# Two graph layers, a mixture of experts and a grouped attention: the weights and masks of the heads built inside the second graph, four open tails, and another last tile

## The chip, the cores and the metric

The kernel runs on one core of a Trainium2 chip. The metric is the device time of one execution in microseconds (us), the median of several runs. The engines have short names in the profile: PE is TensorE (matrix products; PEld is its weight load), DVE is VectorE, ACT is ScalarE, POOL is GpSimd, SP is SyncE, which here only issues transfers. [...]

## The reference, cut to what matters

Input x has 3327 rows of 256 numbers; adj is a 3327 x 3327 matrix of zeros and ones. Everything is float32.

```python
# layer 0
x = x + _L0_gnn_ref(_layernorm(x), adj, W, b)              # graph: normalised adjacency times features
x = x + _L0_ffn_ref(_layernorm(x)[None], ...)[0]           # 8 experts, the best 2 of each row
# layer 1
x = x + _L1_gnn_ref(_layernorm(x), adj, W, a)              # graph with attention weights
x = x + _L1_ffn_ref(_layernorm(x)[None], ...)[0]           # the heads
```

The second graph computes `softmax(where(adj > 0, leaky_relu(e_src + e_dst), -9e15)) @ (x @ W)`. The heads (`_L1_ffn_ref`, 4 heads, 4 queries each, called "experts" e in the kernel, 64 wide):

```python
sx = einsum('bsh,ndh->bnsd', x, hl_w) + hl_b
pad = sx == 0
q = einsum('bnsd,neod->bneso', sx, wq);  k = ... wk;  v = ... wv
att = softmax(einsum('bnesd,bntd->bnest', q, k) * d ** 0.5 + causal)
qkv = where(pad, 0, einsum('bnest,bntd->bnesd', att, v))
gs = softmax(einsum('bnsf,nef->bnse', out, gate_w) + gate_b)      # out is qkv, laid side by side
mixed = einsum('bnsed,bnse->bnsd', out, gs)
hn = layernorm(mixed + resid, ln_g, ln_b)                          # resid is sx
hx = where(pm, 0, relu(where(pm, 0, fx @ fc1.T + fc1_b)))          # fx is hn, pm is fx == 0
hx = layernorm(where(pm, 0, hx @ fc2.T + fc2_b) + fx, fnorm_g, fnorm_b)
fg = softmax(fout @ fgate_w.T)                                     # fout is hx of the four heads
return fout * fg
```

## The kernel before, in words

Rows are cut into 26 tiles of 128. The kernel runs four stages one after the other: the first graph with the experts beside it, the second graph (`graph1`, line 482, until about 974 us of the span), and the heads (`heads`, line 773, from there to the end, 3070.9 us).

**Order.** In the second graph and the heads, instructions are issued through `InOrder` (lines 45 to 100): it adds to each instruction a dependency on the one before it on the same engine. So each engine runs them in the order in which the program writes them, and no scheduler changes that. Since every such instruction is recorded at line 61, the profile's groups are told apart by tile names and shapes.

**The second graph.** Seven blocks of up to four output tiles; a block goes through 26 steps j, one for each source tile. In a step DVE makes u (the larger of two shifted score rows) and p (u masked by the adjacency panel pan), ACT the exponential between them, and PE multiplies p with wh into the accumulators acc. Panels (`panel`, line 668) are fetched by SP, four source tiles at a time; on the diagonal POOL adds the identity (pan<-pan rows). The panel that a step needs is asked for eight steps earlier. POOL also makes the small matrices dg for the next block. Block 3 is the one from about 790.4 to 846.4 us of the span. `finish` (line 712) divides, adds the residual and writes a tile of x to DRAM (xs) through POOL's queue.

**The heads, setup.** At lines 787 to 799 thirteen small weights are loaded with `Net.load` (line 118), which issues on ACT's queue. At lines 810 and 814 twelve parts of wk and wq are loaded on SP's queue. igw, the matrix that turns a head's output back and makes its gate logits, is built by POOL: 32 copies of a 64x64 identity (line 822), and eight transfers of the gate weights on ACT's queue (line 823). own and after, which put the causal mask on the diagonal through a product, are made by POOL's memsets and affine selects (`where`, line 833).

**The heads, loop.** `prepare` (line 880), a generator, makes what a tile t needs: its row norm (xres, prs, xn), the transpose xt, the product sx (psxt in PSUM), then sxd, v, kt, the queries qt and sx. A unit is a tile t and a head h; a unit's keys come in t // 4 + 1 groups g of up to four tiles, and a unit with a group is a chunk. For each chunk: `fill` (PE: scores pqk), `drain` (DVE: from PSUM into sc, with the maximum), `weigh` (ACT: exponential with sum), `values` (SP: loads vr), `turn` (DVE: transposes sc), `attend` (PE: sc times vr into po). After a unit's last group, `over` (line 1074) copies po (ACT) and multiplies by sxd (POOL); in the next chunk `back` (line 1084) makes ptO and fills the head's part of qkv and glp. A running sum of the costs of ACT and DVE (`load`) decides in `empty` (line 856) which of these two makes certain copies out of PSUM.

After head 3, `back` opens the tile's tail (`tail`, line 1146), another generator, which runs in 17 steps between the chunks of later tiles: gate softmax and reciprocals (DVE, ACT), mix of the four experts and residual into fx (POOL), `norm4` (statistics on DVE, power and the rest on POOL), transpose, the two small products ph (PE), mask and sum fo (DVE, POOL), second `norm4`, transpose, pfg and the last softmax, product and sum with x (POOL), output. The main loop (lines 1271 to 1288) advances each open tail and each open `prepare` by one step per chunk, through `run` (line 964); from tile 8 on it leaves out the chunk after a unit's end. Before a tail is opened, open ones are advanced until at most two are left:

```python
                if h == 3:
                    while len(tails) > 2:
                        run(tails)
                    tails.append(tail(u["t"], u["sx"], r["qkv"], r["glp"], r["den"]))
```

At the end, `back(ended)` and `while tails: run(tails)` (lines 1294 and 1295) finish the last tile.

Of the kernel before, what the change touches and what calls it, by code (L numbers as in the profile page):

```python
# [12 lines left out]
F32 = mybir.dt.float32  # L13
BF16 = mybir.dt.bfloat16
# [3 lines left out]
AF = mybir.ActivationFunctionType  # L18
ALU = mybir.AluOpType
AX = mybir.AxisListType  # L20
PSUM = bass.MemoryType.PSUM

P = 128
N = 3327
NT = 26
NP = NT * P
D = 256
# [3 lines left out]
NEG = -1e30  # L31
# [70 lines left out]
class Net:  # L102
# [15 lines left out]
    def load(self, pool, src, shape, name, eng=None, bufs=None):  # L118
        t = pool.tile(shape, F32, name=name, tag=name, bufs=bufs)
        (eng or self.nc.scalar).dma_start(out=t, in_=src)  # L120
        return t

    def load_rows(self, pool, vec, n, name, bufs=None):

        return self.load(pool, vec.partition_broadcast(P), [P, n], name, bufs=bufs)
# [353 lines left out]

        return beside  # L480

    def graph1(self, xs, made):
        tc, a, x = self.tc, self.a, self.x
        nc = InOrder(tc)
        HP = NP // 2

        PARTS = ((0, HP, HP + 9 * P, NP), (0, HP, NP))
        with ExitStack() as ctx:
            one = ctx.enter_context(tc.tile_pool(name="g1", bufs=1))
            panp = ctx.enter_context(tc.tile_pool(name="g1pan", bufs=3))  # L490
            first = ctx.enter_context(ExitStack())
            ps = first.enter_context(tc.tile_pool(name="g1ps", bufs=2, space=PSUM))
# [251 lines left out]
            weights(1)  # L744
            masked(0)
            for k, (b, j) in enumerate(steps):
                if k + 8 in when:
                    load(*when[k + 8])
                if k + 2 < len(steps):
                    if steps[k + 2][1] % 4 == 0 and groups:  # L750
                        panel(*groups.pop(0))
                    weights(k + 2)
                if k + 3 in when:
                    sign(*when[k + 3])
                if k + 1 < len(steps):
                    masked(k + 1)
                gather(k)
                if b and 1 <= j <= len(blocks[b - 1]):
                    finish(blocks[b - 1][j - 1])
                if k in when:  # L760
                    top(*when[k], PARTS[1])
                if b + 1 < len(blocks):
                    if j == 16:
                        dg = shifts(b + 1)
                    if j == 18:
                        pb = rows(b + 1, dg)
                    if j == 21:
                        spread_rows(b + 1, pb)
            for t in blocks[-1]:
                finish(t)  # L770


    def heads(self, xs, vs, out):
        tc, a = self.tc, self.a
        nc = InOrder(tc)
        Q = 32
        with ExitStack() as ctx:
# [6 lines left out]
            ps_o = ctx.enter_context(tc.tile_pool(name="pso", bufs=1, space=PSUM))  # L784
            ps = ctx.enter_context(tc.tile_pool(name="psm", bufs=4, space=PSUM))

            hlt = self.load(one, a["hlt"].rearrange("(k p) o -> p k o", p=P), [P, 2, D], "hlt")
            hlb = self.load(one, a["hlb"], [P, 2], "hlb")
            wv = self.load(one, a["wv"].rearrange("c p o -> p c o"), [P, 2, P], "wv")
            gb = self.load_rows(one, a["gateb"], 16, "gateb")  # L790
            lng = self.load_rows(one, a["lng"][:64], 64, "lng")
            lnb = self.load_rows(one, a["lnb"][:64], 64, "lnb")
            fc1 = self.load(one, a["fc1"], [P, P], "fc1")
            fb1 = self.load(one, a["fb1"], [P, 1], "fb1")
            fc2 = self.load(one, a["fc2"], [P, P], "fc2")
            fb2 = self.load_rows(one, a["fb2"][:64], 64, "fb2")
            fng = self.load_rows(one, a["fng"][:64], 64, "fng")
            fnb = self.load_rows(one, a["fnb"][:64], 64, "fnb")
            fgw = self.load(one, a["fgw"], [P, 2, 4], "fgw")

            wk = one.tile([P, 2, P], F32, name="wk")
            wq = one.tile([P, 2, 2, P], F32, name="wq")
            igw = one.tile([P, 4, 4, 68], F32, name="igw")
            for s in range(2):
                r = ds(64 * s, 64)
                for k in range(2):
                    self.nc.sync.dma_start(  # L810
                        out=wk[r, :, ts(k, 64)], in_=a["wk"][:, r, r].rearrange("c p o -> p c o")
                    )
                    for c in range(2):
                        self.nc.sync.dma_start(
                            out=wq[r, c, :, ts(k, 64)],
                            in_=a["wq"][c, k::2, r, r].rearrange("e p o -> p e o"),
                        )
            for k in range(2):
                r = ds(64 * k, 64)
                for e in range(4):  # L820
                    for h in range(4):
                        nc.gpsimd.tensor_copy(igw[r, h, e, :64], self.ident[r, r])
                    self.nc.scalar.dma_start(
                        out=igw[r, :, e, 64:], in_=a["gatew"][ds(64 * (e % 2), 64), :, e // 2, :]
                    )

            own = [one.tile([P, P], BF16, name=f"own{k}") for k in range(2)]  # L830
            after = [one.tile([P, P], BF16, name=f"after{k}") for k in range(2)]

            def where(t, op, base, sign=1):

                for k in range(2):
                    r = t[ds(64 * k, 64), :]
                    nc.gpsimd.affine_select(
                        out=r, in_=r, compare_op=op, fill=0.0, base=base,
                        pattern=[[sign, P]], channel_multiplier=-2 * sign,
                    )  # L840

            for k in range(2):
                nc.gpsimd.memset(own[k], 1.0)
                nc.gpsimd.memset(after[k], NEG)
            where(own[0], ALU.is_ge, 0)
            where(own[0], ALU.is_ge, 1, -1)
            where(after[0], ALU.is_ge, -2)
            where(own[1], ALU.is_equal, 0)
            where(after[1], ALU.is_equal, -1)

            kt = one.tile([P, 4, NP], F32, name="kt")

# [27 lines left out]
            def prepare(t, res):  # L880
# [14 lines left out]
                nc.vector.tensor_scalar(xn, x, mv[:, 0:1], rs, ALU.subtract, ALU.mult)  # L895
                load["dve"] += 0.35
                yield
                xt = self.work.tile([P, 2, P], F32, tag="xt", name="xt2")
                turned(xn, xt)
                yield  # L900
                pp = ps.tile([P, 2, P], F32, tag="b", name="psxt")
# [172 lines left out]
            def over(u):  # L1074

                u["ot"] = tl.tile([P, 4, P], F32, tag="ot", name="ot", bufs=1)
                nc.scalar.copy(u["ot"].rearrange("p e (q i) -> p q e i", q=4), po)
                nc.gpsimd.tensor_tensor(
                    u["ot"], u["ot"],
                    u["sxd"][:, u["h"] : u["h"] + 1, :].to_broadcast([P, 4, P]), ALU.mult,  # L1080
                )
                load["act"] += 0.6

            def back(u):


                h = u["h"]
                r = ready[u["t"]]
                if h == 0:
                    r["qkv"] = tl.tile([P, 4, 4, 64], F32, tag="qkv", name="qkv", bufs=2)  # L1090
                    r["glp"] = sm.tile([P, 4, 4, 4], F32, tag="glp", name="glp")
                pt = ps.tile([P, 4, 68], F32, tag="b", name="ptO")
                for e in range(4):
                    nc.tensor.matmul(
                        pt[:, e, :], u["ot"][:, e, :], igw[:, h, e, :], start=True, stop=True
                    )
                nc.scalar.copy(r["qkv"][:, h, :, :], pt[:, :, :64])
                nc.scalar.copy(r["glp"][:, h, :, :], pt[:, :, 64:])
                load["act"] += 0.55
                if h == 3:  # L1100
                    while len(tails) > 2:
                        run(tails)
                    tails.append(tail(u["t"], u["sx"], r["qkv"], r["glp"], r["den"]))

# [41 lines left out]
            def tail(t, sx, qkv, glp, den):  # L1146
# [71 lines left out]
                f3 = fo.rearrange("p (h d) -> p h d", h=4)  # L1218
                nc.gpsimd.tensor_tensor(f3, f3, fg.unsqueeze(2).to_broadcast([P, 4, 64]), ALU.mult)
                nc.gpsimd.tensor_tensor(fo, fo, x, ALU.add)  # L1220
                nc.sync.dma_start(out=out[ts(t, P), :], in_=fo)

            units = [dict(t=t, h=h) for t in range(NT) for h in range(4)]
# [529 lines left out]
@with_exitstack  # L1753
def tile_adj_ffn_d2(ctx: ExitStack, tc: tile.TileContext, a: dict, out: bass.AP):
    net = Net(ctx, tc, a)
    dram = ctx.enter_context(tc.tile_pool(name="dram", bufs=1, space=bass.MemoryType.DRAM))
    xs = dram.tile([NP, D], F32, name="xs")

    vs = dram.tile([4, 32, 4 * NT, 64], F32, name="vs")
    with tc.tile_pool(name="feat", bufs=1) as fp:  # L1760


        net.x = fp.tile([P, NT, D], F32, name="x")
        weights = net.graph1_weights(fp)
        with ExitStack() as rows:
            with ExitStack() as moe:
                experts = Experts(moe, net, dram, fp)
                net.graph0(experts, weights)
                experts.run(net.graph1_rows(rows))
            net.graph1(xs, experts)  # L1770
    net.heads(xs, vs, out)


# [76 lines left out]
```

## Time and profile before

| | us |
|---|---|
| median of 3 runs (lowest, highest) | 3073.84 (3071.78, 3076.59) |
| the profiled execution | 3072.57 |
| its span, first to last instruction | 3070.9 |
| PE busy (share of the span) | 2704.3 (88%) |
| PEld | 2009.7 (65%) |
| DVE | 2496.3 (81%) |
| ACT | 1676.9 (55%) |
| POOL | 888.8 (29%) |
| mean granted clock of PE | 0.965 |

A line of the timeline has the start (us from the span's beginning), the busy time, the engine (SPq and ACTq are the queues' DMA issues), the line, the operation, out<-in with the shape, how many instructions are merged, and in brackets how long the engine had been idle and what ended that. A window line has the stretch, its length, each engine's busy time and count, the granted clock of PE (PEclk, 1 is full speed), the DMA engines' mean busy share and GB/s. A share of busy time over the whole span is a mean over stages; which engine sets the pace is read stage by stage.

### The profile page before, as it was taken

The page shows a single profiled execution, that of the slowest core. Times are in us where ns is not written, and L with a number is a line of the kernel's source. Part 1 is how long each engine was busy: PE and PEld are TensorE (multiplying, and loading weights), DVE is VectorE, ACT ScalarE, POOL GpSimd, SP SyncE. Part 2 cuts the span into 40 slices and gives each one's busy share as a digit, 9 for nine tenths or more (in the row PEclk, how much of TensorE's full clock was granted, in tenths as well). Part 3 has the DMA queues.
Part 4 walks back from the last instruction along what each step waited for, and adds up shares of the span by engine and source line. Part 5 has one row for each costly group of instructions (what it writes and reads, how often), then busy time and mean ns, then how long its engine had stood idle before and what let it go on. Part 6 is the DMA issues. An engine that isn't in the chain of part 4 may idle for free.

```text
span 3070.9 us, 126719 instructions
## 1 busy us (share of the span) xinstructions
PE 2704.3 (88%) x54254; PEld 2009.7 (65%) x54254; DVE 2496.3 (81%) x6166; ACT 1676.9 (55%) x4566; POOL 888.8 (29%) x1208
## 2 busy tenths in 40 slices
PE   7999988788887888998999998899989999999884
PEld 5878878666776666666666666666656665666553
DVE  5103643799996678999999999999999999999994
ACT  6410145555553546666666665666656666565663
POOL 6431644711223254432232221222111211111112
PEclk9999999999998889999999999999999999999997
DMA  9994578566763223333333343333333333333431
GB/s 375 356 301 137 185 242 265 182 240 230 262 235 95 66 69 90 109 93 99 110 103 102 111 115 102 103 108 111 108 105 109 111 112 112 111 108 108 118 108 52
DMA packets 258193, 449.80 MB, mean 146 GB/s; under 512 B 58816, under 2 KB 156608, under 8 KB 257504
## 3 DMA queue, kind: packets, MB, share of 16 engines
q1 hardware_dynamic: 241232, 416.77, 44.3%
q0 software_dynamic: 6576, 18.02, 1.6%
q8 instruction: 428, 7.01, 1.0%
q10 hardware_dynamic: 9824, 6.91, 0.8%
q14 instruction: 133, 1.09, 0.1%
HBM read 393.37 MB, written 25.88 MB: 137 GB/s over the span
## 4 chain that ended last, share of the span: by engine, by line
DVE 44%; PE 21%; issue 3%; POOL 2%; ACT 1%; DMA 1%; SPq 0%; ACTq 0%; DVEq 0%; POOLq 0%
DVE sc L61 37%; PE po L61 7%; PE pqk L61 7%; PE acc L61 2%; PE ptO L61 2%; DVE l2mv L61 1%; PE pq L61 1%; DVE l1mv L61 1%; PE psxt L61 1%; DVE fo L61 0%; ACT sc L61 0%; DVE l2st L61 0%; DVE anmax L61 0%; DMA vr<-vs 0%; PE ph L61 0%
## 5 line engine op out<-in xcount | busy, mean ns | idle before, releaser
L61 ACT ACTIVATE sc<-sc,anmax 128x512 f32<-128x512 f32 (+3 forms) x1568 | 1041.2, 671 | 122.5 <-DVE anmax L61 122.3
L61 DVE TENSOR_SCALAR_CACHE_REDUCE sc<-pqk 128x512 f32<-128x512 f32 (+3 forms) x1568 | 897.6, 626 | 51.3 <-PE pqk L61 49.2
L61 PEld LDWEIGHTS po<-sc,vr 32*64 32x64 f32 x43728 | 667.6, 132 | 338.4 <-DVE sc L61 190.5
L61 PE MATMUL po<-sc,vr 32*64 32x128 f32 x43728 | 770.3, 277 | 120.9 <-DVE sc L61 70.4
L61 PE MATMUL pqk<-kt,qt 64*128 64x512 f32 (+3 forms) x3136 | 794.8, 579 | 42.5 <-DVE sc L61 16.9
L61 DVE STREAM_TRANSPOSE sc<-sc 128x2048 f32<-128x2048 f32 (+3 forms) x392 | 816.0, 2082 | 9.3 <-ACT sc L61 9.2
L61 PEld LDWEIGHTS pqk<-kt,qt 64*128 64x128 f32 x3136 | 312.5, 186 | 229.5 <-issue 80.5
L61 PE MATMUL acc<-wh,p 128*128 128x259 f32 x1352 | 309.9, 387 | 33.9 <-DVE p L61 33.9
L61 POOL TENSOR_TENSOR ot<-ot,sxd 128x512 f32<-128x512 f32 x104 | 132.7, 1276 | 658.3 <-ACT ot L61 628.5
L61 PEld LDWEIGHTS acc<-wh,p 128*128 128x128 f32 x1352 | 254.1, 190 | 92.1 <-DVE p L61 51.7
L61 PE MATMUL acc<-y,pan 128*128 128x256 f32 x1352 | 304.1, 385 | 11.1 <-DMA pan<-in_adjt_dram 9.4
L61 ACT ACTIVATION_READ_ACCUMULATOR sc<-sc,anmax 128x1 f32 x1568 | 302.9, 193 | 0.0
L61 PEld LDWEIGHTS acc<-y,pan 128*128 128x128 f32 x1352 | 258.3, 193 | 52.7 <-issue 17.1
L61 ACT ACTIVATE u<-u,d 128x512 f32<-128x512 f32 (+1 forms) x182 | 125.2, 688 | 158.7 <-DVE u L61 158.5
L61 ACT COPY qkv<-ptO 128x256 f32<-128x256 f32 x104 | 38.7, 372 | 226.4 <-PE ptO L61 226.4
L61 DVE SCALAR_TENSOR_TENSOR u<-bc,d 128x512 f32<-128x512 f32 (+1 forms) x182 | 135.3, 744 | 0.1
L61 PE MATMUL ptO<-igw,ot 128*128 128x68 f32 x832 | 116.7, 284 | 20.4 <-DVE sc L61 10.3
L61 DVE SCALAR_TENSOR_TENSOR p<-pan,u 128x512 f32<-128x512 f32 (+1 forms) x182 | 126.0, 692 | 10.6 <-PE acc L61 5.8
L61 PEld LDWEIGHTS ptO<-igw,ot 128*128 128x128 f32 x832 | 102.4, 194 | 39.5 <-issue 19.9
L61 DVE DVE_READ_ACCUMULATOR sc<-pqk 128x1 f32 x1568 | 128.2, 82 | 0.0
L61 ACT ACTIVATE junk<-ar 128x1664 bf16<-128x1664 f32 x52 | 82.7, 1591 | 65.3 <-DMA ar<-in_adj_dram 64.1
L61 PEld LDWEIGHTS <-own 64*128 64x128 bf16 x832 | 53.4, 94 | 92.9 <-issue 80.4
(286 smaller groups left out, 2868.0 us busy)
## 6 DMA issues: line engine op xcount, KB each, us to landing
vr<-vs SPq DMA_DIRECT2D x976, 128.0 KB
ar<-in_adj_dram SPq DMA_DIRECT2D x104, 832.0 KB
vr<-vs SPq DMA_DIRECT2D x544, 96.0 KB
pan<-in_adjt_dram SPq DMA_DIRECT2D x156, 256.0 KB
pan<-in_adjt_dram SPq DMA_DIRECT2D x26, 1024.0 KB
pan<-in_adjt_dram SPq DMA_DIRECT2D x20, 832.0 KB
w1e<-w SPq DMA_DIRECT2D x59, 256.0 KB
took<-places SPq DMA_DIRECT2D x59, 129.0 KB
```

Source lines behind the costliest of these rows:

```text
L61: made = make(*args, **kw)
```

## The change

Four things change.

1. The heads' weights, igw, own and after are made by a new generator, `heads_fixed`, which `graph1` advances by one piece at the start of each step from block 3 on. It has 26 pieces, as many as block 3 has steps, so all of them lie in block 3: pieces 1 to 7 the thirteen small loads, 8 to 11 wk and wq, 12 to 19 igw, 20 and 21 the memsets, 22 to 26 the affine selects. All its transfers are issued on SP's queue. igw takes eight copies of 64x4x64 elements instead of 32 of 64x64. The tiles lie in a new pool, `atf`, opened by the caller of `graph1`.
2. Tile xt2 has one buffer instead of the pool's own number.
3. Up to four tails are left open when a new one is opened, instead of two.
4. The last tile has two tails, `last_tail`, opened after head 1 and after head 3, with two heads each and operations of half the size. The first does its elementwise work on POOL, the second on DVE; power stays on POOL. The last unit's product with sxd is made on DVE as well. The steps of a `last_tail` add nothing to `load`, apart from its softmax.

```diff
-    def graph1(self, xs, made):
+    def graph1(self, xs, made, pool):
         nc = InOrder(tc)
+        fixed = self.heads_fixed(pool, nc)
...
             for k, (b, j) in enumerate(steps):
+                if b > 2:
+                    next(fixed, None)
...
+    def heads_fixed(self, one, nc):
+        def load(src, shape, name):
+            t = one.tile(shape, F32, name=name)
+            nc.sync.dma_start(out=t, in_=src)
+            return t
...
+        hlt = load(a["hlt"].rearrange("(k p) o -> p k o", p=P), [P, 2, D], "hlt")
+        hlb = load(a["hlb"], [P, 2], "hlb")
+        yield
...
+        for k in range(2):
+            r = ds(64 * k, 64)
+            for e in range(4):
+                yield
+                nc.gpsimd.tensor_copy(
+                    igw[r, :, e, :64], self.ident[r, r].unsqueeze(1).to_broadcast([64, 4, 64])
+                )
+                nc.sync.dma_start(
+                    out=igw[r, :, e, 64:], in_=a["gatew"][ds(64 * (e % 2), 64), :, e // 2, :]
+                )
...
+        for k in range(2):
+            yield
+            nc.gpsimd.memset(own[k], 1.0)
+            nc.gpsimd.memset(after[k], NEG)
+        for made in (
+            (own[0], ALU.is_ge, 0), (own[0], ALU.is_ge, 1, -1), (after[0], ALU.is_ge, -2),
+            (own[1], ALU.is_equal, 0), (after[1], ALU.is_equal, -1),
+        ):
+            yield
+            where(*made)
...
-                xt = self.work.tile([P, 2, P], F32, tag="xt", name="xt2")
+                xt = self.work.tile([P, 2, P], F32, tag="xt", name="xt2", bufs=1)
...
-                nc.gpsimd.tensor_tensor(
+                (nc.vector if u is units[-1] else nc.gpsimd).tensor_tensor(
                     u["ot"], u["ot"],
...
-                if h == 3:
-                    while len(tails) > 2:
+                if u["t"] == NT - 1:
+                    if h % 2:
+                        tails.append(last_tail(u["t"], h // 2, u["sx"], r))
+                elif h == 3:
+                    while len(tails) > 4:
                         run(tails)
                     tails.append(tail(u["t"], u["sx"], r["qkv"], r["glp"], r["den"]))
...
+            def last_tail(t, c, sx, r):
+                e = nc.vector if c else nc.gpsimd
+                hs, half = ds(2 * c, 2), ts(c, P)
+                if c == 0:
...
+                    x = r["x"] = tl.tile([P, D], F32, tag="xend", name="xend", bufs=2)
+                    nc.sync.dma_start(out=x, in_=xs[ts(t, P), :])
...
+                def norm2(v, g, b, tag):
...
+                    for h in range(2):
+                        st = sm.tile([P, 6], F32, tag=tag + "lst", name=tag + "lst", bufs=2)
+                        nc.vector.bn_stats(st, v[:, ts(h, 64)])
+                        nc.vector.bn_aggr(mv[:, h, :], st)
...
+                    nc.gpsimd.tensor_tensor(rs, rs, self.nhalf[:, :2], ALU.pow)
+                    yield
+                    for h in range(2):
+                        w = v[:, ts(h, 64)]
+                        nc.vector.tensor_scalar(
+                            w, w, mv[:, h, 0:1], rs[:, h : h + 1], ALU.subtract, ALU.mult
+                        )
+                    yield
+                    e.tensor_tensor(two(v), two(v), rows2(g), ALU.mult)
+                    e.tensor_tensor(two(v), two(v), rows2(b), ALU.add)
...
+                mx = qkv.rearrange("p h e d -> p (h e) d")
+                e.tensor_tensor(mx, mx, gs.unsqueeze(2).to_broadcast([P, 8, 64]), ALU.mult)
+                e.tensor_tensor(qkv[:, :, 0:2, :], qkv[:, :, 0:2, :], qkv[:, :, 2:4, :], ALU.add)
+                e.tensor_tensor(two(fx), qkv[:, :, 0, :], qkv[:, :, 1, :], ALU.add)
+                e.tensor_tensor(fx, fx, sx[:, half], ALU.add)
...
+                pt = ps.tile([P, P], F32, tag="b", name="pt")
+                nc.tensor.transpose(pt, fo, self.ident)
+                nc.scalar.copy(fot, pt)
+                if c == 0:
+                    return
...
+                nc.vector.tensor_tensor(f3, f3, fg.unsqueeze(2).to_broadcast([P, 4, 64]), ALU.mult)
+                nc.vector.tensor_tensor(fo, fo, x, ALU.add)
+                nc.sync.dma_start(out=out[ts(t, P), :], in_=fo)
```

## The prediction

> **What bounds the kernel now.** I read the page's chain of waits first, because the page's busy shares mix three different stages.
>
> ```profile
> DVE 44%; PE 21%; issue 3%; POOL 2%; ACT 1%; DMA 1%; SPq 0%; ACTq 0%; DVEq 0%; POOLq 0%
> ```
>
> DVE and PE carry the chain. Two windows views then ask whether that is so everywhere. Columns after the window: its length, busy time and count of PE, PEld, DVE, ACT, POOL, then PEclk, DMA share, GB/s.
>
> ```profile
> 1122.40:1142.70 20.30, 10.70 (x123) 8.56 (x122) 11.66 (x46) 5.31 (x19) 13.45 (x20) 0.58 0.11 32
> 1143.40:1179.30 35.90, 30.44 (x600) 23.04 (x600) 26.79 (x91) 20.43 (x72) 17.47 (x20) 0.90 0.31 83
> 3033.00:3070.90 37.90, 6.78 (x24) 5.14 (x24) 6.71 (x35) 2.57 (x8) 15.25 (x18) 0.50 0.01 4
> 2700.00:2900.00 200.00, 183.44 (x5451) 122.98 (x5442) 196.46 (x452) 124.59 (x368) 28.11 (x32) 1.00 0.39 111
> 810.00:828.00 18.00, 15.49 (x67) 12.16 (x66) 17.90 (x31) 9.47 (x11) 0.00 (x0) 1.00 0.38 117
> 832.00:846.00 14.00, 14.00 (x62) 11.40 (x61) 12.67 (x21) 10.82 (x14) 0.00 (x0) 1.00 0.87 308
> ```
>
> At 2700 to 2900 (heads, far in) DVE is busy 196.5 of 200 us. The change issues the same work there, so I move nothing in it. Time can only come from the places where no engine is full: the burst at 1122.4, the end from 3033, and the start of the heads, read in the timeline:
>
> ```profile
> 977.04 5.85 POOL L61 COPY igw<-ident 64x64 f32<-64x64 f32 x32 [1.54 <-DMA xs<-x]
> ...
> 986.54 5.25 ACTq L823 DMA_DIRECT2D igw<-in_gatew_dram x8
> 987.17 0.57 POOL L61 TENSOR_TENSOR prs<-prs,nhalf 128x1 f32<-128x1 f32 x1
> 987.77 0.41 DVE L61 TENSOR_SCALAR xn<-xres,pmv,prs 128x256 f32<-128x256 f32 x1 [11.12 <-POOL prs L61]
> ...
> 991.83 0.37 ACT L61 COPY xt<-pt 128x256 f32<-128x256 f32 x1 [21.43 <-DMA igw<-in_gatew_dram]
> ...
> 992.30 2.04 PE L61 MATMUL psxt<-xt,hlt 128*128 128x128 f32 x8 [3.25 <-ACT xt L61]
> ```
>
> Tile 0's layer norm stands at POOL behind 32 small copies, memsets and masks (11.12 us), then its transposed copy stands at ACT behind eight DMA issues.
>
> **Part 1a, the start of the heads.** DVE has written prs by 976.65 (its last operation starts at 976.50 and takes 0.15). With POOL and ACT empty, the rest runs at the trace's own steps: prs 976.75, xn +0.60 = 977.35, transpose +0.62 = 977.97, copy +0.73 = 978.70, psxt +0.42 = 979.12. Today psxt starts at 992.30: **−13.2 us**. I check what is late next: kt and the scores need psxt; the norm's input xres comes from xs, whose last write has landed by then (POOL's copies had waited for it until 977.04). So nothing else stands before psxt; the tile-0 chain after it is unchanged.
>
> **Part 1b, what that work costs in the graph.** It now goes into block 3 (790.4 to 846.4): one step of the generator per graph step. SP takes all 33 DMAs: before, 12 were on SP (8.4 us of issue in 974 to 992) and 21 on ACT (14.7 us), so 23 us of issue. SP's own issues in block 3 are some 38 at 0.43 = 16 us; 39 of 56 us fit. Queued behind them are the panel loads, asked for up to eight graph steps early (8 × 2.15 = 17 us); landing takes about 5, so 12 us of slack. Each new DMA also waits for the one eight places earlier, which at two or three per step is some three steps old. I cost the DMAs at 0; without that cover up to 3.
>
> POOL gets 8 copies (64x4x64 each, in place of 32), 4 memsets and 10 affine selects. Here a wait costs, since DVE has no idle time in 810 to 828. The row for what POOL does to DVE is this pair of the same operation, the first beside POOL's panel work, the second alone:
>
> ```profile
> 802.31 0.94 DVE L61 SCALAR_TENSOR_TENSOR u<-bc,d 128x512 f32<-128x512 f32 x1
> ...
> 812.82 0.74 DVE L61 SCALAR_TENSOR_TENSOR u<-bc,d 128x512 f32<-128x512 f32 x1
> ```
>
> At 802 to 810 eight POOL operations lengthened four u by 0.20, three p by 0.26 and one sg by 0.25: 1.83 us, 0.23 each. The Trainium skill ("SBUF — State Buffer", section "Who interferes with whom") speaks against the change more strongly: a DVE instruction with two SBUF inputs and a GpSimd instruction that reads SBUF exclude each other, and the second is blocked in full. By the row: 8 copies × 0.25 = 2.0; the masks (10 × 0.29 us of POOL, × about 0.57, DVE's lengthening per us of POOL work beside another POOL operation) add 1.6, but fall into 832 to 846, where PE is full (14.00 of 14) and DVE has 1.3 us free. By the rule: 8 × 0.45 + 10 × 0.29 = 6.5. I take the row, **+2.0**, ends 0.5 and 6.5.
>
> **Part 2, four tails.** A tail has 17 steps. Tiles 0 to 3 have four chunks each, one step per chunk, so when tile 4 begins to end its first head three tails hold 12, 8 and 4 steps, and the limit of two forces 5 rounds × 3 = 15 steps in one place: the 20.3 us of the burst, with PE at 10.7 and the clock granted at 0.58. In it PE and DVE wait for each other by way of POOL:
>
> ```profile
> 1136.85 0.69 PE L61 MATMUL pt<-ident,fo 128*128 128x128 f32 x2 [3.90 <-POOL fo L61]
> ...
> 1138.43 0.42 DVE L61 TENSOR_TENSOR fo<-ph,fb 128x256 f32<-128x256 f32 x1 [4.51 <-PE ph L61]
> ```
>
> It is the only one: from tile 4 on eight rounds run per tile, and tails drain faster than they open. With four allowed none is forced, and the same steps lie between the chunks of tiles 4 and 5. The work does not vanish: of DVE's 11.66 us about 8.3 are tails', POOL's 13.45 all. The next 35.9 us have 9.1 us of DVE, 18.4 of POOL and 5.5 of PE free. Gain's ends: 0, or a little below (everything is again on the path, rival B), and 13 (all but attention's own 3.4 us of DVE and half of the tails' 8.3). I see no loss beyond that: no operation is added, and tails four steps apart hold at most three fx, which is how many there are. DVE's idle time in the burst is 20.3 − 11.66 = 8.6; I take it as what goes, rounded down for steps that still wait: **−8**.
>
> **Part 3, the last tile.** Between ACT's last copy of po (3032.90) and the end lie 38.0 us in a single file, POOL 15.25 of it:
>
> ```profile
> 3033.57 1.26 POOL L61 TENSOR_TENSOR ot<-ot,sxd 128x512 f32<-128x512 f32 x1 [26.41 <-ACT ot L61]
> ...
> 3039.74 1.90 POOL L61 TENSOR_TENSOR qkv<-qkv,gss 128x1024 f32<-128x1024 f32 x1 [4.91 <-DVE gss L61]
> ...
> 3050.28 0.69 PE L61 MATMUL pt<-ident,fx 128*128 128x128 f32 x2 [13.42 <-POOL fx L61]
> ```
>
> Only the second half (two heads, on DVE) is left behind the last po. Start to start, with DVE's duration for the shape (128x512: 0.69 against POOL's 1.26) and half sizes: po copy 0.67, ot multiply 0.74 (was 1.31), ptO 2.0, its copies 0.5, gate 2.5 (was 2.4: two operations of the first half come between), mix and residual 2.1 (was 4.9), statistics 1.06 (1.72), power on POOL, normalise, scale and shift 1.9 (3.95), transpose and copy 0.7 (1.15), ph 0.67 (1.26), relu and mask 0.85 (1.1), second ph 0.67 (1.22), fo 1.2 (1.8), statistics 1.06 (1.7), norm 1.9 (3.95), transpose and copy 0.7 (1.15), pfg 1.06, softmax 1.25, multiply and add 1.05 (1.44), output 3.5 as now: 26.0, so −12.0. Against it: the first half is opened after head 1 and runs 12 of its 17 steps between the chunks of heads 2 and 3. Its first five steps (gate 2.2 us of DVE) fall before 3000.6, where DVE is still full, and push the last head by about 2.2; later DVE has only transposes (2.3 of 3.9 us per chunk). Its small ACT copies wait for PE while exponentials stand behind them; ACT is 10 us ahead there, so 0.3. **−9.5**.
>
> The second xt2 buffer's loss costs nothing: the next use is a whole tile later.
>
> **Sum.** −13.2 + 2.0 − 8 − 9.5 = −28.7 on the profiled execution's 3072.57 (span 3070.9 and 1.67 around it): 3043.9. The median of the runs is 1.27 above that execution, so **3045 us**.
>
> **Rivals.**
> - *Burst work only moves* (B): tiles 4 and 5 turn out bound by POOL to DVE to PE as the burst is. For it: POOL needs 13.45 + 17.47 = 31 us in about 40. Against: 9 us of DVE idle beside it. Gain 0: 3053.
> - *The graph pays in full* (C): the lock as the rule has it (+4.5), or panels late by up to 3, seen as DVE's p waiting for a pan DMA. For it: DVE full at 810 to 828. 3050.
> - *The burst goes nearly whole* (D), −13: the freed steps fit into PE's and DVE's gaps. 3040.
> - *SP runs over* (E, the other side): panel loads queue behind the 33 DMAs. Decides when each holds SP for (56 − 16 + 29) / 33 = 2.1 us, waits for earlier DMAs included: then block 3 is 29 us longer and all is lost, 3075 or more. The rows show 0.3 to 0.72 us each.
> - *No change of order*: nothing of parts 1 to 3 is left to a scheduler that could undo it; every engine's queue is held in program order. I give it nothing.
>
> **How the numbers follow.** Likeliest (A, sum as above, 3040 to 3050 of its own) 0.52; B 0.17; C 0.14; D 0.13; E 0.04. B and C together give 3058, D with a cheap graph 3037; the range 3035 to 3057 leaves out E, part of B with C and of D. A difference of 0.2% (6.1 us) is about what a measurement of this kernel can tell from no change. A to D are all faster by more: 0.96; E is split, 0.01 within and 0.03 slower.
>
> **What would show it.** Right: the first psxt some 5 us after the graph's last x instead of 18, and DVE's xn without a wait for POOL prs; no stretch in tile 4 with the clock at 0.58; about 26 us from the last copy of po to the end, with DVE under the fx and fo rows; block 3 of 58 us. Wrong: p rows waiting on pan DMAs, u and p at double length beside igw (C, E); DVE rows that wait for PE or POOL spread over 1120 to 1180 (B); ACT's fxt copy late with exponentials behind it in the last head. A slower exponential stream there would also take from part 3.

## The result, and the profile after

The changed kernel takes 3040.39 us (median of 4 runs, 3033.66 to 3042.51), the kernel before 3074.34 (4 runs, 3071.78 to 3076.59): a ratio of 0.9886, with a 95% interval of 0.9868 to 0.9904, so some 34 us less, between 29 and 41. On another chip, later, it was 3044.30 against 3079.74, a ratio of 0.9893 (0.9878 to 0.9908). Forecast were 3045, with 3035 to 3057.

The profiled execution of the changed kernel is its fastest run (3033.66, span 3032.0), so its span is 38.9 below that of before, more than the medians. The shares in the chain of waits have moved to DVE; PE, POOL and issue lost:

```profile
DVE 48%; PE 19%; issue 2%; ACT 1%; DMA 0%; POOL 0%; SPq 0%; DVEq 0%; POOLq 0%; ACTq 0%
```

The start of the heads in the timeline. DVE's wait for POOL falls from 11.12 us to 0.69, and ACT's copy follows the transpose (pt) instead of the load issues:

```profile
975.50 0.57 POOL L61 TENSOR_TENSOR prs<-prs,nhalf 128x1 f32<-128x1 f32 x1 [1.28 <-DVE prs L61]
976.10 0.41 DVE L61 TENSOR_SCALAR xn<-xres,pmv,prs 128x256 f32<-128x256 f32 x1 [0.69 <-POOL prs L61]
...
977.42 0.37 ACT L61 COPY xt<-pt 128x256 f32<-128x256 f32 x1 [8.44 <-PE pt L61]
977.84 2.08 PE L61 MATMUL psxt<-xt,hlt 128*128 128x128 f32 x8 [0.46 <-ACT xt L61]
```

Next come three stretches in windows cut at the same events in both kernels: block 3 of the graph (from the first xs issue of one block to that of the next), then tile 4 and tile 5 (each from the product of ot with sxd of the tile before's last head to that of its own). Before:

```profile
790.42:846.44 56.02, 49.06 (x214) 39.47 (x213) 54.45 (x86) 30.61 (x36) 12.70 (x14) 1.00 0.72 257
1120.31:1179.31 59.00, 43.94 (x799) 33.74 (x796) 41.22 (x146) 27.19 (x96) 33.01 (x42) 0.80 0.24 66
1179.31:1221.06 41.75, 38.51 (x907) 27.67 (x904) 39.63 (x120) 27.40 (x91) 19.97 (x22) 1.00 0.38 104
```

After, with the end (from ACT's last copy of po) as a fourth:

```profile
788.05:845.14 57.09, 49.07 (x214) 39.40 (x213) 56.32 (x86) 30.50 (x36) 28.38 (x36) 1.00 0.80 264
1105.76:1149.11 43.35, 37.94 (x786) 28.66 (x784) 39.36 (x132) 26.54 (x94) 28.57 (x36) 0.92 0.29 83
1149.11:1194.82 45.71, 41.33 (x919) 29.71 (x918) 41.65 (x134) 28.08 (x94) 25.01 (x29) 0.96 0.35 101
3006.60:3032.00 25.40, 6.09 (x21) 4.38 (x21) 13.30 (x55) 2.61 (x9) 3.03 (x5) 0.52 0.02 6
```

Tile 4 takes 43.35 us instead of 59.00 with nearly the same DVE work in it (39.36 against 41.22). Tile 5 has 2.0 us more of DVE and takes longer. The end takes 25.40 instead of 38.0, with POOL at 3.0 instead of 15.3. In the end's timeline the elementwise rows are DVE's:

```profile
3007.22 0.69 DVE L61 TENSOR_TENSOR ot<-ot,sxd 128x512 f32<-128x512 f32 x1 [3.71 <-ACT ot L61]
...
3012.72 0.83 DVE L61 TENSOR_TENSOR qkv<-qkv,lgss 128x512 f32<-128x512 f32 x1
...
3017.74 0.48 PE L61 MATMUL pt<-ident,fx 128*128 128x128 f32 x1 [4.20 <-DVE fx L61]
```

Cut at common events, the 38.9 us of the two profiled executions split so: 2.4 ahead of block 3, where the code is the same; block 3 −1.1; from the last xs issue to psxt 17.94 − 4.76 = 13.2; nothing from there to the end of tile 3 (0.1); tile 4 15.65; tile 5 −4.0; tile 6 1.9; tiles 7 to 24 −1.1; tile 25 up to the last po copy −0.8; the end 12.6. So the change itself gave about 36 in this pair; the 2.4 is not its doing. Stretches whose code is the same differ from execution to execution by more than that: over the profiled executions of all kernels here, block 3 began between 787.8 and 796.2 us, and tiles 7 to 24 took between 1636.7 and 1648.1. So a stage is compared below by its own length, and a whole kernel by its runs, not by one span.

### The profile page after: what moved, and what is told of

It is laid out like the page before. It is cut to its first block, busy times and chain, and to the rows that moved or that the text cites. A ratio compares the mean times of both kernels' runs of the same rounds, so it can differ in the third digit from the quotient of the medians.

```text
span 3032.0 us, 126726 instructions
## 1 busy us (share of the span) xinstructions
PE 2702.8 (89%) x54254; PEld 2004.2 (66%) x54254; DVE 2506.5 (83%) x6203; ACT 1678.2 (55%) x4570; POOL 886.5 (29%) x1178
## 4 chain that ended last, share of the span: by engine, by line
DVE 48%; PE 19%; issue 2%; ACT 1%; DMA 0%; POOL 0%; SPq 0%; DVEq 0%; POOLq 0%; ACTq 0%
DVE sc L61 40%; PE po L61 7%; PE pqk L61 6%; PE acc L61 2%; PE ptO L61 1%; DVE fo L61 1%; DVE l2mv L61 1%; DVE l1mv L61 1%; ACT sc L61 0%; PE pq L61 0%; DVE anmax L61 0%; DVE gl L61 0%; DVE l2st L61 0%; PE psxt L61 0%; DVE l1st L61 0%
## 5 line engine op out<-in xcount | busy, mean ns | idle before, releaser
L61 DVE STREAM_TRANSPOSE sc<-sc 128x2048 f32<-128x2048 f32 (+3 forms) x392 | 816.1, 2082 | 12.9 <-ACT sc L61 12.9
L61 PEld LDWEIGHTS acc<-wh,p 128*128 128x128 f32 x1352 | 254.2, 191 | 92.7 <-DVE p L61 51.9
## 6 DMA issues: line engine op xcount, KB each, us to landing
vr<-vs SPq DMA_DIRECT2D x976, 128.0 KB, 2.6
pan<-in_adjt_dram SPq DMA_DIRECT2D x26, 1024.0 KB, 10.7
```

Source lines behind the costliest of these rows:

```text
L61: made = make(*args, **kw)
```

## The experiments

The lengths that decide, from each kernel's profiled execution, in us. "Head start" is from the graph's last xs issues (one row of two in the timeline, counted from its start) to psxt, "tile 25" from its first head's product with sxd to ACT's last copy of po.

| kernel | block 3 | head start | tile 4 | tile 5 | tile 25 | end |
|---|---|---|---|---|---|---|
| before | 56.02 | 17.94 | 59.00 | 41.75 | 90.7 | 38.0 |
| changed | 57.09 | 4.76 | 43.35 | 45.71 | 91.5 | 25.4 |
| p1_only | 57.13 | 4.44 | 59.40 | 41.76 | 91.3 | 38.0 |
| p2_only | 56.12 | 17.81 | 43.72 | 44.00 | 91.6 | 38.0 |
| p3_only | 56.10 | 18.15 | 59.00 | 41.78 | 91.8 | 24.9 |
| dma_only | 56.09 | 9.13 | 59.06 | 41.77 | 90.8 | 38.0 |
| pool_only | 56.88 | 14.47 | 59.38 | 41.75 | 89.8 | 38.0 |
| catchup2 | 57.15 | 4.66 | 41.66 | 42.14 | 92.3 | 25.3 |
| last_pool | 57.10 | 4.72 | 43.80 | 46.93 | 93.2 | 27.4 |
| late_pieces | 57.00 | 4.48 | 43.71 | 46.33 | 94.4 | 25.3 |
| copies_twice | 57.85 | 4.76 | 43.53 | 43.97 | 93.2 | 25.3 |
| earlier | 56.08 | 1.31 | 43.68 | 46.31 | 92.6 | 25.3 |
| after_again | 57.07 | 4.73 | 43.79 | 43.98 | 92.7 | 25.2 |

### Each part alone

**p1_only**: the kernel before with the setup inside the graph.

```diff
-                if u["t"] == NT - 1:
-                    if h % 2:
-                        tails.append(last_tail(u["t"], h // 2, u["sx"], r))
-                elif h == 3:
-                    while len(tails) > 4:
+                if h == 3:
+                    while len(tails) > 2:
...
-                (nc.vector if u is units[-1] else nc.gpsimd).tensor_tensor(
+                nc.gpsimd.tensor_tensor(
```

(The diff is against the changed kernel.)

> The heads' setup moved into the second graph (and one xt2 buffer), the rest as before. My theory, from the two profiles: psxt starts 4.8 us after the graph's last xs issue instead of 17.9 (-13.2), block 3 lasts 57.1 instead of 56.0 (+1.1), about 1.3 is given back in tile 0: -11, so 3063. The burst of 20 us and the end of 38 us stay. Rival: the heads' first tiles take the gain back (DVE sets the pace in them anyway): under -5.

Measured: 0.9960 of before (0.9946 to 0.9974) on its chip, which is −12.3 of 3083. The stages are as expected, block 3 and head start both. The rival (under 5 us) is out. From psxt to the end of tile 3 this execution took 130.8 us, the one before 128.0; but p2_only, which leaves the start as it was, took 131.2 there and the changed kernel 127.9, so no giving back can be read from it.

**p2_only**: only the limit.

```diff
-                    while len(tails) > 2:
+                    while len(tails) > 4:
```

> Only the limit of open tails, four instead of two. My theory: the stretch from the product of tile 3's last head to that of tile 4's last head shrinks from 59 to about 43.5 us, tile 5 becomes some 4 us longer, the rest as before: -11, so 3063. Rival B (work only moves): under -3. Rival D: -15 or more, nothing of it given back in tile 5.

Measured: 0.9957 (0.9941 to 0.9974), −13.3. Windows of tile 4 and tile 5:

```profile
1129.19:1172.91 43.72, 38.70 (x786) 29.13 (x783) 39.47 (x132) 26.39 (x94) 28.59 (x35) 0.92 0.31 82
1172.91:1216.91 44.00, 39.66 (x919) 28.72 (x916) 41.44 (x134) 27.99 (x94) 25.00 (x30) 1.00 0.39 105
```

Here tile 5 has the full granted clock (1.00), as in the kernel before (41.75 us). Compared so, tile 4 gives 15.3 and tile 5 takes 2.2 back: 13.1 net. DVE is busy for 80.9 us in the two tiles, before and after; its idle time fell from 19.9 to 6.8, which is the gain. Rival B (the work only moves) is out: the work did move, the time did not come back. Rival D as put here (15 or more, nothing given back) isn't met; the 13 that the prediction gave it is.

This size holds where the clock is full. Over tiles 4 to 6 together the kernel before takes 148.3 us, and the seven profiled executions with the limit of four save between 8.9 (last_pool) and 14.9 (p2_only, after_again) of it. The difference goes with the clock: in three of the seven the granted clock was 0.93 in tiles 5 and 6, while the six with the limit of two had 1.00 in tile 5 and 0.96 or 1.00 in tile 6. The last section works out where such dips come from; the higher limit opens tile 5 to them, which the prediction did not see. The median of p2_only's four runs is 12.9 below that of before.

**p3_only**: only the last tile, in the kernel before (`last_tail` and the last product with sxd as in the change, one xt2 buffer, the limit of two kept for the other tiles).

```diff
-                if h == 3:
+                if u["t"] == NT - 1:
+                    if h % 2:
+                        tails.append(last_tail(u["t"], h // 2, u["sx"], r))
+                elif h == 3:
                     while len(tails) > 2:
```

> Only the last tile's two half tails (and one xt2 buffer), the limit for other tiles still two. My theory: from ACT's last copy of po to the end 25.4 us instead of 38.0 (-12.6), the last two heads about 0.8 later: -11.8, so 3062. Rival: the half tail between the chunks costs DVE and ACT more than 2 us in heads 2 and 3, gain under 9.

Measured: 0.9959 (0.9945 to 0.9973), −12.6. The end is 24.9. The three parts' gains add up to 38.2, against 33 to 35 for the whole by its ratios (29 to 41 by the interval). By medians the parts give 10.7, 12.9 and 12.0, together 35.6, against 34.0 and 35.4. There is no sign that one part lives off another, but this isn't measured closely enough to exclude a few us.

### What the setup had waited for, and what it costs in the graph

**dma_only**: all transfers (DMA) on SP inside the graph; POOL's work in the heads' own code. Against p1_only:

```diff
-                nc.gpsimd.tensor_copy(
-                    igw[r, :, e, :64], self.ident[r, r].unsqueeze(1).to_broadcast([64, 4, 64])
-                )
                 nc.sync.dma_start(
                     out=igw[r, :, e, 64:], in_=a["gatew"][ds(64 * (e % 2), 64), :, e // 2, :]
...
+            for k in range(2):
+                r = ds(64 * k, 64)
+                for e in range(4):
+                    nc.gpsimd.tensor_copy(
+                        igw[r, :, e, :64], self.ident[r, r].unsqueeze(1).to_broadcast([64, 4, 64])
+                    )
```

(The memsets and masks move with the copies.)

> Only the 33 transfers are moved into the graph, on SP's queue; POOL's eight wide copies, memsets and masks stay at the start of the heads; no other part of the change. If POOL's work is what lengthens block 3, it lasts 56.0 us again; if the transfers do it (panels late), 57.1. At the start of the heads ACT's wait for its eight issues is gone, POOL's stays: eight copies of about 0.5, memsets 0.6 and masks 3.3 end at about 985, psxt starts about 11 to 15 us after the last xs issue instead of 17.9: -4, so 3070. If the issues on ACT had been the whole wait, -11 like the whole part.

Measured: 0.9971 (0.9961 to 0.9982), −8.9, and the head start 9.13: twice the gain that I expected. The reason shows in the copies into the tile igw:

```profile
L61 POOL COPY igw<-ident x8: 399/408/417, 489.4 to 493.9; 64x256 f32<-64x256 f32 x8
```

The copies didn't run at the start of the heads at all but at 489 us, in the stage before the second graph. I read this from the program: the heads begin a new chain of order, so nothing held the first instructions on POOL back, and the tile had already been allocated. Only memsets and masks still stood before prs:

```profile
982.65 0.21 POOL L61 MEMSET own<- 128x128 bf16 x1 [1.51 <-DMA xs<-x]
...
986.78 0.57 POOL L61 TENSOR_TENSOR prs<-prs,nhalf 128x1 f32<-128x1 f32 x1
987.39 0.41 DVE L61 TENSOR_SCALAR xn<-xres,pmv,prs 128x256 f32<-128x256 f32 x1 [5.10 <-POOL prs L61]
```

So this kernel isolates less of the start than it was made for: it takes away ACT's issues and the copies at once (8.8 us of the 13.2), and the memsets and masks that are left hold the other 4.4. What it does settle is block 3: with all 33 transfers in it and none of POOL's work, it takes 56.09. The transfers cost nothing measurable (0.07); with POOL's work alone (pool_only, next) it takes 56.88. The 1.07 is POOL's, to within 0.2.

**pool_only**: the other half, POOL's pieces in the graph, all transfers on their old queues. Against the kernel before:

```diff
+        for _ in range(11):
+            yield
+        igw = one.tile([P, 4, 4, 68], F32, name="igw")
...
+                nc.gpsimd.tensor_copy(
+                    igw[r, :, e, :64], self.ident[r, r].unsqueeze(1).to_broadcast([64, 4, 64])
+                )
...
-                    for h in range(4):
-                        nc.gpsimd.tensor_copy(igw[r, h, e, :64], self.ident[r, r])
```

> The kernel before, with only POOL's copies, memsets and masks moved into the graph; all 33 transfers stay at the start of the heads on ACT's and SP's queues. My theory (two waits side by side; ACT's issues end last): DVE's xn comes 10 us earlier, but ACT's copy xt still stands behind the issues, psxt 17.5 us after the last xs issue instead of 17.9, block 3 57.1: 0.7 slower than before. Rival (POOL's 11.12 us is the wait that counts): psxt 8 us earlier.

One run, 3079.70, no difference that one run can show. The timeline:

```profile
982.22 0.41 DVE L61 TENSOR_SCALAR xn<-xres,pmv,prs 128x256 f32<-128x256 f32 x1 [0.69 <-POOL prs L61]
...
992.81 0.33 ACTq L120 DMA_DIRECT2D fgw<-in_fgw_dram  x1
993.19 0.37 ACT L61 COPY xt<-pt 128x256 f32<-128x256 f32 x1 [18.08 <-DMA fnb<-in_fnb_dram]
993.66 2.05 PE L61 MATMUL psxt<-xt,hlt 128*128 128x128 f32 x8 [10.40 <-ACT xt L61]
```

xn waits for POOL only 0.69 us, and psxt gains 3.5 of 13.2. Its remaining wait is ACT's, behind thirteen load issues (the eight for igw now come after the copy, which is why the gain isn't 0.4 as I expected). The two waits stood side by side: with POOL's gone, ACT's still holds psxt. The rival, POOL alone, is out. The opposite case, ACT's issues gone and all of POOL's work left, has no run, since dma_only lost the copies too.

**late_pieces**: two pieces a step from step 13 on.

```diff
-                if b > 2:
-                    next(fixed, None)
+                if b > 2 and j > 12 or b > 3:
+                    for _ in range(2):
+                        next(fixed, None)
```

> The changed kernel with the pieces of the setup made two per step from step 13 of block 3 on, so that POOL's copies and masks fall into the steps in which PE is full. If the +1.07 us of block 3 are from DVE being full at the place, block 3 is back at 56.0 to 56.3. If what POOL costs does not depend on the place, 57.1. If the transfers cost when they come closer together, more.

One run, 3046.34. Block 3 is 57.00, so my theory of the place falls. DVE's rows from the timeline, beside copies (first), beside masks (the next two), and the only wait of the block:

```profile
836.76 0.88 DVE L61 SCALAR_TENSOR_TENSOR p<-pan,u 128x512 f32<-128x512 f32 x1
...
840.58 0.77 DVE L61 SCALAR_TENSOR_TENSOR u<-bc,d 128x512 f32<-128x512 f32 x1
841.27 0.77 DVE L61 SCALAR_TENSOR_TENSOR p<-pan,u 128x512 f32<-128x512 f32 x1
...
844.89 0.69 DVE L61 SCALAR_TENSOR_TENSOR p<-pan,u 128x512 f32<-128x512 f32 x1 [0.76 <-PE acc L61]
```

DVE shows no other wait in the block, although PE is busy throughout its last steps. So DVE has no free time in the block except near its end, where it absorbs part of what POOL adds: its idle time in the block is 1.57 us in the kernel before, 0.77 in the changed one and 1.04 here.

**copies_twice**: sixteen copies instead of eight (the second of each pair writes the same).

```diff
-                nc.gpsimd.tensor_copy(
-                    igw[r, :, e, :64], self.ident[r, r].unsqueeze(1).to_broadcast([64, 4, 64])
-                )
+                for _ in range(2):
+                    nc.gpsimd.tensor_copy(
+                        igw[r, :, e, :64], self.ident[r, r].unsqueeze(1).to_broadcast([64, 4, 64])
+                    )
```

> The changed kernel with each of the eight igw copies made twice (the second writes the same). By the row of the prediction (0.23 us of DVE per operation of POOL) block 3 grows from 57.1 to about 59; by what the changed kernel's trace shows (u, p and sg 0.13 to 0.20 longer beside a copy that itself takes 1.2 us) to 58.2; if the whole of a copy were lost to DVE, by 8 x 0.4 or more, 60.3 upward.

One run, 3043.64. Block 3 is 57.85 (window below, beside 57.09): eight more copies cost 0.76, 0.1 each, and 1.06 of DVE's busy time (57.38 against 56.32).

```profile
788.04:845.89 57.85, 49.06 (x214) 39.54 (x213) 57.38 (x86) 30.54 (x36) 35.25 (x45) 1.00 0.79 260
```

All three sizes that I had written (+1.9, +1.1, +3.2) were too high, the last by far.

### Why four tails give time

**catchup2**: the limit of two, but two steps per chunk in tiles 0 to 3, so that none is forced.

```diff
-                    while len(tails) > 4:
+                    while len(tails) > 2:
...
-                    run(tails)
+                    for _ in range(2 if u["t"] < 4 else 1):
+                        run(tails)
```

> The changed kernel with the limit of two put back, but open tails advanced twice per chunk in tiles 0 to 3, so that no tail is forced at tile 4. My theory (what the change removes is the forced rounds, not the number of tails): the stretch from tile 3's last product to tile 4's is 44 us or less as with four tails, tile 5 is not longer than before (about 42), tiles 1 to 3 take up to 5 more than their 92: about as fast as the changed kernel, within 5. Rival (it is the number of open tails that fills the gaps): the 59 us come back, 14 slower than the changed kernel.

Measured: 0.9906 (0.9889 to 0.9922), the changed kernel 0.9893 on another chip: 4 us apart by the ratios, within their intervals. Tiles 1 to 3 (first line), 4 and 5 in windows:

```profile
1019.80:1123.41 103.61, 86.15 (x1440) 63.99 (x1436) 74.94 (x235) 52.90 (x172) 52.30 (x56) 0.85 0.25 69
1123.41:1165.07 41.66, 37.99 (x788) 27.95 (x789) 35.44 (x121) 26.41 (x93) 20.39 (x23) 0.96 0.32 86
1165.07:1207.21 42.14, 38.61 (x911) 27.93 (x906) 40.02 (x120) 27.53 (x92) 19.96 (x22) 1.00 0.36 101
```

Tiles 4 and 5 are as I said; tiles 1 to 3 take 103.6, where the kernel before takes 92.6, 11 more and not "up to 5". Both theories are half right. The forced rounds can be avoided without a higher limit, but the steps then cost 11 us in tiles 1 to 3. Measured against tiles 4 and 5 of this kernel (83.8 us, which have 5.4 us less of DVE work), the same steps cost 17 us in the forced place (100.8) and 4 when four tails may wait (p2_only, 87.7). The higher limit is what lets them wait. That DVE is busy for only 75 of the 104 us in tiles 1 to 3 shows that idle time there is not room for a step. I take it that with four short chunks per tile each inserted step stands in a chain of waits; that was not tested apart.

### Half a tail, or another engine

**last_pool**: the second half tail's elementwise work on POOL.

```diff
-                e = nc.vector if c else nc.gpsimd
+                e = nc.gpsimd
```

> The changed kernel with the second half tail's elementwise work on POOL as well (the last product with sxd and the last two operations stay on DVE). My theory: most of the gain is from halving. One product 0.83 to 1.27, one sum 0.42 to 0.72, six of 0.29 to 0.45, and some changes of engine: from ACT's last copy of po to the end 27.5 to 28 instead of 25.4. Rival: it is DVE that makes it, 31 or more.

Measured: 0.9891 (0.9872 to 0.9911), and the end is 27.41, close to the 27.5 to 28 expected:

```profile
3022.59:3050.00 27.41, 5.23 (x21) 3.58 (x21) 10.32 (x47) 2.60 (x9) 7.47 (x13) 0.56 0.02 6
```

Of the 12.6 us at the end 10.6 are from having half of the work there (with the last product with sxd and the last two operations on DVE), 2.0 from DVE for the rest.

### Further in the same direction

**earlier**: POOL's setup outside the graph's order, so that the scheduler places it before the graph; the norm of tile 0 of the heads in the graph's last block.

```diff
-                nc.gpsimd.tensor_copy(
+                self.nc.gpsimd.tensor_copy(
...
+        for _ in range(54):
+            yield
+        x = self.x[:, 0, :]
...
+        nc.vector.bn_stats(st, x)
+        nc.vector.bn_aggr(mv, st)
+        nc.vector.tensor_scalar(rs, mv[:, 1:2], 1e-5, None, ALU.add)
+        yield
+        nc.gpsimd.tensor_tensor(rs, rs, self.nhalf[:, :1], ALU.pow)
+        yield
+        nc.vector.tensor_scalar(self.first, x, mv[:, 0:1], rs, ALU.subtract, ALU.mult)
```

> The changed kernel, with two steps moved further: POOL's copies, memsets and masks outside the second graph's order, so that they come before it, where POOL has nothing else to do; and the norm of the heads' tile 0 inside the graph's last block (from x in SBUF) instead of after it. My theory: block 3 at 56.0 (-1.05), psxt 1.5 to 2 us after the last xs issue instead of 4.8 (-3): 4 less than the changed kernel. Rival: xn is not what psxt waits for (PSUM or PE's weights are): psxt as before, only -1. If POOL's early work collides with the first graph, that stage becomes longer by 1 or more.

> The changed kernel itself, on the same chip as the next two. By the sum of its stages (head start -13.3, block 3 +1.05, tiles 4 to 6 -10 to -15, the end -12.6 with 1.6 given back in tile 25) 33 to 40 less than before, -36 in the middle. If the parts' own medians add up (-12.3, -13.3, -12.6): -38. If the first chip's -34 was right in itself: -34.

Measured on one chip: earlier 3041.57, 0.9881 of before (0.9862 to 0.9900); the changed kernel 3044.30, 0.9893 (0.9878 to 0.9908). The medians don't tell them apart. The stages do: block 3 is 56.08 and the head start 1.31, together 4.4 less than in after_again. The timeline:

```profile
975.61 1.14 POOL L61 DMA_DIRECT2D xs<-x  x2 [7.18 <-DVE rd L61]
976.05 0.41 PE L61 MATMUL pt<-ident,xn 128*128 128x128 f32 x2 [1.03 <-DVE x L61]
...
976.92 1.16 PE L61 MATMUL psxt<-xt,hlt 128*128 128x128 f32 x8 [0.46 <-ACT xt L61]
```

POOL's copies and masks now run from 484.8 to 497.8 us. Whether they cost something there stays open: block 3 began at 791.6 in this execution and at 787.8 in after_again, but the executions without them range from 787.8 to 796.2.

## Why the prediction was right

The direction, the range and each part's sign held; the time was 4.6 us lower than forecast. One term of the sum, the four tails, was much too small (8 against 13): the time is the 3040 that the forecast gave for rival D, at a chance of 0.13, and the total lay within the range because the range was wide enough to hold it. By its steps:

- **Start of the heads, −13.2**: measured 13.2 in the two profiles. The text put the two waits one after the other; they ran side by side, and removing POOL's alone was worth only 3.5.
- **Block 3, +2.0**: measured 1.07. DVE's busy time in the block rose by 1.87 (54.45 to 56.32), half of the 3.6 worked out (2.0 for the copies, 1.6 for the masks), and 0.8 of it went into DVE's idle time. The cover was credited to the masks, by their place; the place has no part in it (late_pieces). By the rule of the Trainium skill ("SBUF — State Buffer", "Who interferes with whom"), 6.5 of DVE's time would have been lost if DVE had been the one blocked every time. In the trace both give way, POOL more: a copy takes 0.41 us beside the lighter DVE work at 489 us (dma_only) but 0.74 to 0.86 beside u and p and 2.05 beside sg, while u and p grow by 0.13 and 0.20 and sg by 0.2. The rule does not say that DVE is the one to be blocked. The copies in the changed kernel (shortest, median and longest in ns):

```profile
L61 POOL COPY igw<-ident x8: 742/852/2059, 813.1 to 830.8; 64x256 f32<-64x256 f32 x8
```

- **Transfers on SP, 0**: right (dma_only, 56.09 against 56.02). Of rival C's late panels (up to 3 us) and of E's 29 there was nothing.
- **Four tails, −8**: measured 15.3 in tile 4 less 2.2 in tile 5, 13.1 at equal clock. This term was mis-sized. The step that failed is "DVE's idle time in the burst ... I take it as what goes": it left the moved 8.3 us of DVE work on the path, though the same paragraph gives 9.1 us of free DVE time in the rest of tile 4, and that is where most of it went (tile 5 took 1.8). Rival D had the right number for this term. In the executions with the lower clock less of it was left (8.9 at the least, over tiles 4 to 6).
- **The last tile, −9.5**: the end gave 12.6 (forecast 12.0). Tile 25 costs more, as foreseen: 0.8 in the two profiles, and over the eight profiled executions with half tails (91.5 to 94.4) and the five without (89.8 to 91.6) 92.7 against 90.8 on average, so about 1.9, where I had 2.5.

With these sizes, at the full clock, the sum is −13.2 + 1.1 − 13.1 − 12.6 + 1.9 = −36, between the forecast's −28.7 and the −38.9 of the profiled pair; the medians have −34 and −35.4. One figure among the rivals doesn't come out: D with the graph at its low end of 0.5 is 3038.5, not 3037; nothing rests on it.

## What to carry to other kernels

Where a burst is taken apart, its gain isn't limited to the bottleneck engine's idle time in the burst: the idle time of the place where the work goes counts too (here 19.9 us of DVE's in tiles 4 and 5 together, of which 13.1 were won, against 8.6 in the burst alone). The last tile's serial chain was shortened far more by doing half of it early than by giving it to a faster engine (10.6 us against 2.0). And if two queues both delay the first use of something, price each wait to the same event before crediting either.

## What the runs showed of the hardware

- Beside DVE's u and p, which have two inputs from SBUF, POOL's copies took twice as long (0.74 to 0.86 us against 0.41), and its masks too (2.62 / 4 = 0.66 us against 1.35 / 4 = 0.34); a copy that met DVE's sg (1.88 us alone) took 2.05 us. DVE lost 0.03 to 0.2 us per operation. I had looked only at DVE's side.
- DMA issues held up the compute behind them on the same engine: in pool_only the input of ACT's copy xt was there by 983.25 us (the transpose's start, 982.84, and its 0.41), but the copy started at 993.19, after the thirteenth issue. The same transfers on SP's queue, inside the graph, left block 3 as it was (56.02 and 56.09 us).
- The granted clock of PE in tiles 5 and 6 differed between executions of the same code. Tile 5 of the changed kernel had 0.96 and took 45.71 us in one execution, and 1.00 and 43.98 in another (after_again, first line). In earlier, with the same code in this tile, it had 0.93 and took 46.31 (second line). Tile 6 took between 45.67 us at 1.00 and 48.65 at 0.93 (after_again and earlier).

```profile
1150.58:1194.56 43.98, 39.65 (x919) 28.70 (x915) 41.42 (x134) 27.98 (x94) 24.99 (x30) 1.00 0.37 105
1149.27:1195.58 46.31, 42.36 (x919) 30.95 (x915) 41.59 (x134) 28.06 (x94) 24.98 (x29) 0.93 0.35 99
```

The records of the clock show what such a dip is: half the clock for 3.41 us or a multiple of it, and within an execution all dips begin whole multiples of 3.41 us apart. So the time can be cut into windows of 3.41 us on that grid. In tiles 4 to 6 of the thirteen executions, of the windows at the full clock in which PE was busy for less than 1.9 us, 31 of 32 were followed by half the clock; of those above 2.1 us, 1 of 424; in between, 7 of 14. The same stretch of tile 5, with the window after it, in earlier (first two lines) and in after_again:

```profile
1155.20:1158.61 3.41, 1.76 (x86) 1.40 (x84) 3.07 (x15) 3.11 (x11) 2.00 (x4) 1.00 0.03 9
1158.61:1162.02 3.41, 3.30 (x16) 2.98 (x16) 3.40 (x8) 0.49 (x2) 1.05 (x1) 0.50 0.78 221
1157.06:1160.47 3.41, 1.97 (x87) 1.54 (x87) 3.10 (x15) 2.57 (x9) 2.18 (x3) 1.00 0.13 43
1160.47:1163.89 3.42, 3.06 (x24) 2.28 (x26) 3.38 (x8) 2.26 (x8) 0.52 (x2) 1.00 0.79 220
```

Where the grid falls decides whether a thin stretch of PE's work lies in one window or is split over two. With four tails the thinnest window of tile 5 has 1.71 to 2.06 us of PE in the seven executions, with two 2.23 to 2.60 in the six. So the change brought tile 5 to where dips begin: four of the seven have one there, none of the six. That this grid and this boundary hold elsewhere isn't shown.
